# Columns of maxima become rows by a VectorE transpose and GpSimd copies, in place of TensorE products with the identity

## The chip, the cores and the metric

The kernel runs on one core of one Trainium2 chip. The metric is the device time in microseconds of one execution; times are medians of several runs. Engines are named as in the profile: PE is TensorE's matmul and PEld its weight load, DVE is VectorE, ACT is ScalarE, POOL is GpSimd, SP is SyncE, whose queue issues most DMAs.

## The reference

The input x has 4096 tokens of 256 features, all float32. There are two residual stages: causal attention with 16 heads of 16 features, then a feed-forward part with five linear maps.

```
def attn(x):                      # x: [1, 4096, 256]
    q, k, v = split(x @ w_attn + b_attn, 3)      # 16 heads of 16
    logits = q @ k^T * 16 ** -0.5
    logits = where(causal, logits, -inf)
    return softmax(logits) @ v @ w_proj + b_proj

def ffn(x):
    h = silu((x @ w1^T) * s1) * ((x @ w2^T) * s2)
    h = gelu((h @ h1^T) * sh1)
    h = gelu((h @ h2^T) * sh2)
    return (h @ w3^T) * s3

x = x + layernorm(attn(layernorm(x)))
x = x + layernorm(ffn(layernorm(x)))
```

The softmax subtracts each query's true maximum. The change touches only how this maximum gets from where it is found to where it is used.

## The kernel before, in words

**Tiling.** Queries come in 8 blocks j of 512 tokens (QB), each of 4 tiles t of 128 (P). The 16 heads form 4 groups g of 4; a group is two pairs pr of two heads i. The work of the attention is a list of 32 items (j, g), counted here from 0. Item (j, g) has 4(j+1) steps kt, one for each 128 keys up to the diagonal.

**Two passes.** An item needs its maxima before its scores. `MaxUnit` computes, with queries on the partitions, 128 x 512 logits of two heads into two PSUM banks `pm` (L596; three such banks in a ring) and reduces each on DVE to one column of `mx` (L630; L634 with the causal mask on the diagonal; if `hold` is set, ACT first copies one bank to SBUF at L615 and DVE reduces the copy at L619). After the last unit of an item, DVE takes the maximum over key blocks with the sign turned, `neg` (L647), rounds it, `high` (L653), and writes `high` and the rest `neg - high` into columns of `mcol` (L657, L658): 4 heads, 2 parts, 4 query tiles. `ScoreUnit` then computes the logits the other way round, with keys on the partitions and queries along the free axis (L701): a first product with q and k and a second that adds the negative maximum, as a product of a matrix of ones with a row tile `mrow`, which must hold the maxima along the free axis. ACT takes the exponential of two heads at once (L716), POOL zeroes what lies above the diagonal with an affine select in the last four steps of an item (L721), and four products with the values (L751, each issued twice in the trace) add to `av`, one step later than their scores.

**Columns to rows, before.** `to_rows` (L661) multiplies each of the four 128 x 128 tiles of `mcol` with the identity on PE (L666) into a PSUM tile `pmt`, taken from the ring of two that the scores use as well, and ACT copies it to SBUF as `mrow` (L675). In `mcol` the two heads of a pair lie 64 columns apart, so that in `mrow` they lie on the two halves of the partitions, where the two products of L701 read them; all other columns are zero. `ones[pr]` (L405) has ones in the four rows that belong to pair pr.

**Order.** All engines run in program order; the order is written out by hand (L893 on). In step kt of item n the program issues the first `MaxUnit` of a pair, the two `ScoreUnit`s, the second `MaxUnit`, the values of the step before, and then `rows_of`, background work (`bg.pace`: layernorm and projections of other blocks) and a piece of `halve_weights` on POOL (L786). The maxima run about one item ahead of the scores and three steps more (`LEAD`); in items with g < 3 of the middle blocks up to four pairs more are drawn ahead beside the background work (`unit_beside`, L857). `issue` (L842) puts a finished item into `rows_due` with the time `now + 4`, where `now` goes up by 2 per step, so its rows are made two steps later. `lent` notes that ACT was used beside the exponentials; the next step then does not hold.

Of the kernel before, what the change touches and what calls it, by code (L numbers as in the profile page):

```python
# [10 lines left out]
F32 = mybir.dt.float32  # L11
F32R = mybir.dt.float32r
AF = mybir.ActivationFunctionType
ALU = mybir.AluOpType
AX = mybir.AxisListType
PSUM = bass.MemoryType.PSUM

P = 128
QB = 512
NT = QB // P  # L20
NEG = -1.0e30
# [46 lines left out]
def sandwich_kernel(  # L68
# [19 lines left out]
    nc = tc.nc  # L88
# [6 lines left out]
    G = H // 4  # L95
    NB = S // QB
    DC = D // P
    FC = F // P
    SCALE = HD ** -0.5

    const = ctx.enter_context(tc.tile_pool(name="const", bufs=1))
    lent = []
# [4 lines left out]
    stat = ctx.enter_context(tc.tile_pool(name="stat", bufs=3))  # L107

    def rows(src, j):
        return src[j * QB : (j + 1) * QB, :].rearrange("(t p) d -> p t d", p=P)  # L110

    def load_block(j, src=x):
        t = xpool.tile([P, NT, D], F32, tag="x", name=f"x{j}")
        nc.sync.dma_start(out=t, in_=rows(src, j))
        return t


    x1 = [
        scratch.tile([QB, D], F32, tag=f"x1_{j}", name=f"x1_{j}") for j in range(NB)
    ]  # L120
# [10 lines left out]

    ident = const.tile([P, P], F32, tag="ident", name="ident")
    make_identity(nc, ident)
# [54 lines left out]
    def piece(tag, name, dtype=F32):  # L188
        return pieces.tile([P, QB], dtype, tag=tag, name=name)

# [12 lines left out]
    def load_pieces(src, tiles):  # L203
        for (c, o), t in tiles.items():
            nc.sync.dma_start(
                out=t.bitcast(F32), in_=src[c * P : (c + 1) * P, o * QB : (o + 1) * QB]
            )
# [139 lines left out]
    with ExitStack() as actx:  # L347
        aw = actx.enter_context(tc.tile_pool(name="aw", bufs=1))
        kv = actx.enter_context(tc.tile_pool(name="kv", bufs=1))
        wk2 = actx.enter_context(tc.tile_pool(name="wk2", bufs=2))  # L350
# [10 lines left out]
        def two_banks(name):  # L361
            return ps_s.tile([P, 2, QB], F32, tag="s", name=name)
# [17 lines left out]
        for d in range(DC):  # L380
# [10 lines left out]
        nc.scalar.dma_start(out=bqk, in_=b_attn[0 : 2 * D].rearrange("(s p) -> p s", p=P))  # L391
        nc.vector.tensor_scalar(bqk[:, 0:DC], bqk[:, 0:DC], SCALE, None, ALU.mult)

        two = aw.tile([P, 2], F32, tag="two", name="two")
        nc.vector.tensor_reduce(
            two,
            ident.rearrange("p (i pr e) -> p pr i e", i=2, pr=2)[:, :, :, 0:2],
            AX.XY,
            ALU.add,
        )  # L400
        identr = aw.tile([P, P], F32R, tag="identr", name="identr")
        nc.vector.tensor_copy(identr, ident)
        ones = [aw.tile([P, P], F32R, tag=f"ones{pr}", name=f"ones{pr}") for pr in range(2)]
        for pr in range(2):
            nc.vector.tensor_copy(ones[pr], two[:, pr : pr + 1].to_broadcast([P, P]))  # L405
# [16 lines left out]
        vb, qT, mT = [], {}, {}  # L422
# [161 lines left out]
        class MaxUnit:  # L584
# [19 lines left out]
            def finish(self, hold=False):  # L604
                j, g, t, c, pr = self.at
                n = self.n
                heads = list(self.ps.items())
                if hold:


                    h, ps = heads.pop(0)
                    held = const.tile(
                        [P, QB], F32, tag=f"xT0{'hl'[c % 2]}", name=f"held_{j}_{g}_{t}_{c}"
                    )
                    nc.scalar.copy(held[:, 0:n], ps[:, 0:n])  # L615
                    heads.append((h, held))
                for h, ps in heads:
                    if not self.diagonal and hold and ps is held:
                        nc.vector.tensor_scalar(  # L619
                            held[:, 0:n],  # L620
                            held[:, 0:n],
                            -3.0e38,
                            None,
                            ALU.max,
                            ALU.max,
                            accum_out=self.mx[:, h, c : c + 1],
                        )
                        continue
                    if not self.diagonal:
                        nc.vector.tensor_reduce(  # L630
                            self.mx[:, h, c : c + 1], ps[:, 0:n], AX.X, ALU.max
                        )
                        continue
                    nc.vector.tensor_tensor_reduce(  # L634
                        out=ps[:, 0:n],
                        in0=ps[:, 0:n],
                        in1=mask[:, QB - n : QB],
                        scale=1.0,
                        scalar=-3.0e38,
                        op0=ALU.add,  # L640
                        op1=ALU.max,
                        accum_out=self.mx[:, h, c : c + 1],
                    )
                if not (self.diagonal and pr == 0):
                    return False
                neg, mcol = self.neg, self.mcol
                nc.vector.tensor_reduce(  # L647
                    neg[:, t, :], self.mx[:, :, 0 : j + 1], AX.X, ALU.max, negate=True
                )
                if t < NT - 1:  # L650
                    return False
                high = stat.tile([P, NT, 4], F32R, tag="high", name=f"high_{j}_{g}")
                nc.vector.tensor_copy(high, neg)  # L653

                col = mcol.rearrange("p t (i pr e) -> p t pr i e", i=2, pr=2)
                by_pair = [a.rearrange("p t (pr i) -> p t pr i", pr=2) for a in (neg, high)]
                nc.vector.tensor_copy(col[:, :, :, :, 0], by_pair[1])  # L657
                nc.vector.tensor_tensor(col[:, :, :, :, 1], *by_pair, ALU.subtract)  # L658
                return True

            def to_rows(self):  # L661

                j, g = self.at[:2]
                ps = two_banks(f"pmt_{j}_{g}")[:, 0, :]
                for t in range(NT):
                    nc.tensor.matmul(  # L666
                        ps[:, t * P : (t + 1) * P],
                        lhsT=self.mcol[:, t, :],
                        rhs=identr,
                        start=True,  # L670
                        stop=True,
                    )
                mrow = wk2.tile([P, QB], F32R, tag="mrow", name=f"mrow_{j}_{g}")
                lent.append(True)
                nc.scalar.copy(mrow, ps)  # L675
                mT[j, g] = mrow

        class ScoreUnit:

# [85 lines left out]
                        bg.add(("project", j), project(j, room), PROJECT)  # L765


        mcols = [aw.tile([P, NT, P], F32R, tag=f"mcol{i}", name=f"mcol{i}") for i in range(2)]
        for mcol in mcols:
            nc.gpsimd.memset(mcol.bitcast(F32), 0.0)  # L770

        PW = 256
        fit = aw.tile([P, PW], F32, tag="fit", name="fit")
# [66 lines left out]
        rows_due = deque()  # L840

        def issue(unit, **how):  # L842
            unit.products()
            done = unit.finish(**how)
            if done is True:
                rows_due.append((now + 4, unit))
            return done

        def rows_of(limit):
            while rows_due and rows_due[0][0] <= limit:  # L850
                rows_due.popleft()[1].to_rows()

# [2 lines left out]
        def unit_beside():  # L857
            j, g = item
            if not begun_pair and 1 <= j < NB - 1 and g < G - 1 and len(ahead) < NT:
                begun_pair.extend(next(stream))  # L860
                ahead.append(1)
            if begun_pair:
                issue(MaxUnit(*begun_pair.pop(0)))
# [6 lines left out]
        ps = two_banks("pb")[:, 0, 0:D]  # L870
        for c in range(DC):
            nc.tensor.matmul(
                ps,
                lhsT=bv[:, c : c + 1].to_broadcast([P, P]),
                rhs=wp[:, c, :],
                start=(c == 0),
                stop=(c == DC - 1),
# [10 lines left out]
        while issued < first[1] + LEAD:  # L888
            for args in next(stream):
                issue(MaxUnit(*args))  # L890
            issued += 1
        rows_of(now + 4)
        for n, (j, g) in enumerate(items):  # L893
            if n + 2 < len(items):
# [21 lines left out]
            for kt in range(count[n]):  # L916
# [7 lines left out]
                if pairs:  # L924
                    unit = MaxUnit(*pairs[0][0])
# [16 lines left out]
                if j > 0 and kt % 4 == 2 and kt < NT * j:  # L942
                    next(halving, None)
            rows_of(now + 2)
            if n == len(items) - 2:
                count_low()
# [253 lines left out]
```

## Time and profile before

| | us |
|---|---|
| median of 3 runs | 2411.34 |
| lowest and highest | 2408.91, 2411.72 |
| the profiled execution | 2409.51 |
| its span, first to last instruction | 2407.8 |
| PE busy | 2332.1 |
| DVE busy | 1772.5 |
| ACT busy | 1460.8 |
| POOL busy | 564.3 |
| attention, until about | 1750 |

Busy time is the time in which an engine has at least one instruction under way. A row of the profile names the line, the engine, the operation, the tiles written and read, shapes and count; behind the bar stand the busy time, the mean duration, and the idle time of the engine just before, with what ended it. Rows of the timeline start with the time since the span began and the duration; instructions of one kind in a row are merged. The value in brackets is the idle time before, with the instruction that ended it.

### The profile page before, as it was taken

The page shows a single profiled execution, that of the slowest core. Times are in us where ns is not written, and L with a number is a line of the kernel's source. Part 1 is how long each engine was busy: PE and PEld are TensorE (multiplying, and loading weights), DVE is VectorE, ACT ScalarE, POOL GpSimd, SP SyncE. Part 2 cuts the span into 40 slices and gives each one's busy share as a digit, 9 for nine tenths or more (in the row PEclk, how much of TensorE's full clock was granted, in tenths as well). Part 3 has the DMA queues.
Part 4 walks back from the last instruction along what each step waited for, and adds up shares of the span by engine and source line. Part 5 has one row for each costly group of instructions (what it writes and reads, how often), then busy time and mean ns, then how long its engine had stood idle before and what let it go on. Part 6 is the DMA issues. An engine that isn't in the chain of part 4 may idle for free.

```text
span 2407.8 us, 40664 instructions
## 1 busy us (share of the span) xinstructions
PE 2332.1 (97%) x15237; PEld 1413.8 (59%) x15237; DVE 1772.5 (74%) x4053; ACT 1460.8 (61%) x1995; POOL 564.3 (23%) x898
## 2 busy tenths in 40 slices
PE   4899999999999999999999999999999999999998
PEld 2545545545554555455555455544388888888887
DVE  1667897997997999799999998987056546544653
ACT  1437776777786888688789887976822222222221
POOL 2324343333343224322422323000001100000000
PEclk8879999999999999999999999999999999999999
DMA  4443434334334323524223232111031000000000
GB/s 143 162 147 132 152 119 154 122 96 139 103 115 131 109 91 106 167 84 151 75 70 94 80 111 65 61 58 62 1 104 45 27 1 18 18 16 3 18 9 11
DMA packets 134831, 202.77 MB, mean 84 GB/s; under 512 B 14913, under 2 KB 59585, under 8 KB 134625
## 3 DMA queue, kind: packets, MB, share of 16 engines
q1 hardware_dynamic: 132672, 198.75, 25.5%
q8 instruction: 122, 2.00, 0.3%
q10 hardware_dynamic: 1776, 1.18, 0.3%
q14 instruction: 85, 0.69, 0.1%
q0 software_dynamic: 176, 0.15, 0.1%
HBM read 137.91 MB, written 62.13 MB: 83 GB/s over the span
## 4 chain that ended last, share of the span: by engine, by line
PE 84%; DVE 7%; DMA 3%; issue 2%; POOL 2%; ACT 1%; SPq 1%; ACTq 0%; POOLq 0%; DVEq 0%
PE av L751 20%; PE z L1056 19%; PE s L701 18%; PE pm L596 15%; DVE mx L630 3%; PE za L1056 2%; PE zb L1056 2%; PE pyf L1138 2%; DVE pm L634 2%; PE py L254 1%; PE pk L439 1%; PE pmt L666 1%; DMA k<-k 1%; SPq L462 1%; DMA k<-lok 1%
## 5 line engine op out<-in xcount | busy, mean ns | idle before, releaser
L716 ACT ACTIVATE e<-s 128x1024 f32<-128x1024 f32 (+3 forms) x1175 | 1038.2, 936 | 168.1 <-PE s L701 155.5
L630 DVE TENSOR_REDUCE mx<-pm 128x1 f32<-128x512 f32 x1545 | 989.0, 685 | 136.7 <-PE pm L596 103.5
L596 PE MATMUL pm<-k,q 64*128 64x512 f32 (+3 forms) x2304 | 587.8, 443 | 22.6 <-DVE mx L630 9.4
L596 PEld LDWEIGHTS pm<-k,q 64*128 64x128 f32 x2304 | 310.3, 187 | 502.8 <-DVE mx L630 349.7
L751 PE MATMUL av<-e,v 128*32 128x512 f32 (+3 forms) x4608 | 579.2, 573 | 1.8 <-POOL e L721 1.7
L701 PE MATMUL s<-q,k 64*128 64x512 f32 (+3 forms) x2304 | 467.1, 390 | 5.7 <-ACT xT L547 1.2
L701 PE MATMUL s<-mrow,ones 64*128 64x512 f32 (+3 forms) x2304 | 454.3, 380 | 0.0
L1123 ACT ACTIVATE fb<-z,sh 128x512 f32<-128x512 f32 x128 | 88.3, 690 | 364.6 <-PE z L1056 339.3
L634 DVE CUSTOM_DVE_ANT_0 pm<-pm,mask 128x128 f32<-128x128 f32 (+3 forms) x506 | 236.6, 514 | 72.1 <-PE pm L596 68.3
L701 PEld LDWEIGHTS s<-q,k 64*128 64x128 f32 x2304 | 231.4, 187 | 76.6 <-issue 18.2
L701 PEld LDWEIGHTS s<-mrow,ones 64*128 64x128 f32 x2304 | 236.1, 187 | 36.3 <-ACT mrow L675 0.5
L721 POOL TENSOR_SCALAR_AFFINE_SELECT e<-e 128x256 f32<-128x256 f32 x256 | 102.7, 409 | 583.7 <-ACT e L716 580.6
L1056 PE MATMUL z<-hb_0h,h 128*128 128x512 f32 x512 | 199.3, 389 | 0.0
L1056 PE MATMUL z<-hb_0l,h 128*128 128x512 f32 x512 | 199.2, 389 | 0.0
L615 ACT COPY held<-pm 128x512 f32<-128x512 f32 x253 | 148.6, 588 | 52.1 <-PE pm L596 30.2
L751 PEld LDWEIGHTS av<-e,v 128*32 128x32 f32 x4608 | 91.8, 108 | 147.2 <-issue 131.2
L176 POOL TENSOR_TENSOR rstd<-ve,neghalf 128x4 f32<-128x4 f32 (+1 forms) x22 | 20.8, 945 | 644.4 <-DVE ve L174 618.3
L619 DVE TENSOR_SCALAR_CACHE_REDUCE held<-held 128x512 f32<-128x512 f32 x247 | 167.0, 676 | 0.0
L1023 DVE CAST hb_1h<-fb 128x512 fp32r<-128x512 f32 x64 | 27.3, 427 | 155.3 <-ACT fb L1123 155.3
L1100 ACT ACTIVATE sl<-za,s 128x512 f32<-128x512 f32 x64 | 44.1, 690 | 120.1 <-PE za L1056 60.9
L1056 PEld LDWEIGHTS z<-hb_0l,h 128*128 128x128 f32 x512 | 96.1, 188 | 19.9
L1056 PEld LDWEIGHTS z<-hb_0h,h 128*128 128x128 f32 x512 | 96.1, 188 | 19.9
(251 smaller groups left out, 2522.7 us busy)
## 6 DMA issues: line engine op xcount, KB each, us to landing
k<-k SPq DMA_DIRECT2D x288, 256.0 KB
q<-q SPq DMA_DIRECT2D x64, 256.0 KB
x<-in_x_dram SPq DMA_DIRECT2D x16, 512.0 KB
k<-hik SPq DMA_DIRECT2D x32, 256.0 KB
k<-lok SPq DMA_DIRECT2D x32, 256.0 KB
q<-hiq SPq DMA_DIRECT2D x32, 256.0 KB
q<-loq SPq DMA_DIRECT2D x32, 256.0 KB
avd<-av_sb SPq DMA_DIRECT2D x32, 256.0 KB
```

The lines of the kernel that those rows point to most:

```text
L596: nc.tensor.matmul(ps[:, 0:n], lhsT=qT[j, g][pr][r, t * P : (t + 1) * P], rhs=kT[G * j + g, c, pr][r, 0:n], start=True, stop=True,)
L615: nc.scalar.copy(held[:, 0:n], ps[:, 0:n])
L619: nc.vector.tensor_scalar(held[:, 0:n], held[:, 0:n], -3.0e38, None, ALU.max, ALU.max, accum_out=self.mx[:, h, c : c + 1],)
L630: nc.vector.tensor_reduce(self.mx[:, h, c : c + 1], ps[:, 0:n], AX.X, ALU.max)
L634: nc.vector.tensor_tensor_reduce(out=ps[:, 0:n], in0=ps[:, 0:n], in1=mask[:, QB - n : QB], scale=1.0, scalar=-3.0e38, op0=ALU.add, op1=ALU ...
L701: nc.tensor.matmul(self.ps[i][:, self.q0 :], lhsT=(self.k, ones[pr])[m][r, :], rhs=(qT[j, g][pr], mT[j, g])[m][r, self.q0 :], start=(m == ...
L716: nc.scalar.activation(e[:, at : at + n, q0:], ps[:, :, q0:], AF.Exp)
L721: nc.gpsimd.affine_select(out=at, in_=at, compare_op=ALU.is_ge, fill=0.0, base=0, pattern=[[0, 2], [1, P]], channel_multiplier=-1,)
L751: nc.tensor.matmul(self.av[h * HW : (h + 1) * HW, q0:], lhsT=vb[kt // NT][:, kt % NT, o : o + HW], rhs=es[h // 2][:, h % 2, q0:], start=(k ...
L1056: nc.tensor.matmul(ps, lhsT=w[c], rhs=single(part[:, c, :]), start=(c == 0 and i == 0), stop=(c == kc - 1 and i == parts - 1),)
L1123: nc.scalar.activation(h, z, AF.Gelu, scale=sc[:, oc : oc + 1])
L1138: nc.tensor.matmul(ps[:, 0:D], lhsT=single(part[:, c, t * P : (t + 1) * P]), rhs=(w3_r if halves else w3_sb)[:, c, :], start=(c == 0 and i ...
```

## The change

DVE now transposes the columns in 32 x 32 blocks and POOL puts the blocks into their places. `mcol` shrinks to 32 columns per query tile, of which 8 are used; the transpose turns each block of 32 queries by 32 columns in place, so that queries 32b to 32b+31 end up on partitions 32b to 32b+31 as rows of columns. Four copies on POOL, one for each b, move 32 partitions by 128 elements into 32 partitions of a row tile; they are done twice, for partitions 0 to 31 and 64 to 95 (i = 0 and 1), the first four after the step in which the maxima are finished, the others one step later. The row tiles are now two fixed ones, zeroed once. Both halves hold the rows of all four heads; `ones` is rearranged so that each half picks its own. The identity in the products' rounded type (`identr`), the four products, the copy on ACT and its entry in `lent` are gone.

```diff
+        halves = aw.tile([P, 2, 2], F32, tag="halves", name="halves")
+        for i in range(2):
+            at = (P // 2 + 4) * i
+            nc.vector.tensor_reduce(
+                halves[:, i, :],
+                ident[:, at : at + 4].rearrange("p (pr e) -> p pr e", pr=2),
+                AX.X,
+                ALU.add,
+            )
         two = aw.tile([P, 2], F32, tag="two", name="two")
-        nc.vector.tensor_reduce(
-            two,
-            ident.rearrange("p (i pr e) -> p pr i e", i=2, pr=2)[:, :, :, 0:2],
-            AX.XY,
-            ALU.add,
-        )
-        identr = aw.tile([P, P], F32R, tag="identr", name="identr")
-        nc.vector.tensor_copy(identr, ident)
+        nc.vector.tensor_tensor(two, halves[:, 0, :], halves[:, 1, :], ALU.add)
...
-                col = mcol.rearrange("p t (i pr e) -> p t pr i e", i=2, pr=2)
+                col = mcol[:, :, 0:8].rearrange("p t (i pr e) -> p t pr i e", i=2, pr=2)
                 by_pair = [a.rearrange("p t (pr i) -> p t pr i", pr=2) for a in (neg, high)]
                 nc.vector.tensor_copy(col[:, :, :, :, 0], by_pair[1])
                 nc.vector.tensor_tensor(col[:, :, :, :, 1], *by_pair, ALU.subtract)
+                self.turned = stat.tile([P, NT, TB], F32, tag="turned", name=f"turned_{j}_{g}")
+                nc.vector.transpose(self.turned, mcol.bitcast(F32))
                 return True
 
-            def to_rows(self):
+            def to_rows(self, i):
                 j, g = self.at[:2]
-                ps = two_banks(f"pmt_{j}_{g}")[:, 0, :]
-                for t in range(NT):
-                    nc.tensor.matmul(
-                        ps[:, t * P : (t + 1) * P],
-                        lhsT=self.mcol[:, t, :],
-                        rhs=identr,
-                        start=True,
-                        stop=True,
-                    )
-                mrow = wk2.tile([P, QB], F32R, tag="mrow", name=f"mrow_{j}_{g}")
-                lent.append(True)
-                nc.scalar.copy(mrow, ps)
-                mT[j, g] = mrow
+                mT[j, g] = mrow = mrows[g % 2]
+                at = slice(i * P // 2, i * P // 2 + TB)
+                row = mrow[at, :].rearrange("c (t b q) -> c t b q", t=NT, q=TB)
+                for b in range(P // TB):
+                    nc.gpsimd.tensor_copy(row[:, :, b, :], self.turned[b * TB : (b + 1) * TB, :, :])
...
-        mcols = [aw.tile([P, NT, P], F32R, tag=f"mcol{i}", name=f"mcol{i}") for i in range(2)]
-        for mcol in mcols:
-            nc.gpsimd.memset(mcol.bitcast(F32), 0.0)
+        mcols = [aw.tile([P, NT, TB], F32R, tag=f"mcol{i}", name=f"mcol{i}") for i in range(2)]
+        mrows = [aw.tile([P, QB], F32R, tag=f"mrow{i}", name=f"mrow{i}") for i in range(2)]
+        for zero in mcols + mrows:
+            nc.gpsimd.memset(zero.bitcast(F32), 0.0)
...
             if done is True:
-                rows_due.append((now + 4, unit))
+                rows_due.extend(((now + 2, unit, 0), (now + 4, unit, 1)))
             return done
 
         def rows_of(limit):
             while rows_due and rows_due[0][0] <= limit:
-                rows_due.popleft()[1].to_rows()
+                _, unit, i = rows_due.popleft()
+                unit.to_rows(i)
```

`TB` is 32.

More of the change, by code (lines that the diff above doesn't have):

```diff
@@ L18 @@
 P = 128
+TB = 32
 QB = 512
```

## The prediction

> **What bounds the kernel now.** I read the views in this order: busy time by stage, the groups by form, then the timeline of one engine at a time around single row products. The stages first (time, then busy us and instructions of PE, PEld, DVE, ACT, POOL, the granted clock, DMA):
>
> ```profile
> core 0: us, PE busy (x) PEld busy (x) DVE busy (x) ACT busy (x) POOL busy (x), PEclk, DMA share, GB/s
> 300.00:600.00 300.00, 294.30 (x2134) 150.67 (x2134) 257.70 (x614) 224.10 (x321) 110.75 (x183) 1.00 0.39 126
> 600.00:900.00 300.00, 298.25 (x2204) 154.46 (x2200) 269.45 (x607) 236.28 (x322) 100.36 (x158) 1.00 0.35 110
> ```
>
> In the attention PE is never idle and DVE is busy nine tenths of the time; POOL has two thirds free. But a busy PE may be waiting inside its queue, so the place itself decides. Here is the end of the maxima of item 30 (a pair of query block and head group; 32 of them, counted from 0). DVE, then PE, then POOL:
>
> ```profile
> 1579.05 0.18 DVE L658 TENSOR_TENSOR mcol<-neg,high 128x16 fp32r<-128x16 f32 x1
> 1579.13 2.48 DVE L630 TENSOR_REDUCE mx<-pm 128x1 f32<-128x512 f32 x4
> 1582.41 0.69 DVE L630 TENSOR_REDUCE mx<-pm 128x1 f32<-128x512 f32 x1 [0.81 <-PE pm L596]
> ```
> ```profile
> 1579.87 0.49 PE L596 MATMUL pm<-k,q 64*128 64x512 f32 x1 [0.40 <-DVE mx L630]
> 1580.30 1.06 PE L751 MATMUL av<-e,v 128*32 128x512 f32 x8
> 1581.29 0.66 PE L666 MATMUL pmt<-identr,mcol 128*128 128x128 f32 x4
> 1581.88 0.50 PE L596 MATMUL pm<-k,q 64*128 64x512 f32 x2
> ```
> ```profile
> 1579.93 0.41 POOL L721 TENSOR_SCALAR_AFFINE_SELECT e<-e 128x256 f32<-128x256 f32 x1 [1.13 <-ACT e L716]
> 1580.63 0.41 POOL L721 TENSOR_SCALAR_AFFINE_SELECT e<-e 128x256 f32<-128x256 f32 x1 [0.29 <-ACT e L716]
> 1583.38 0.92 POOL L721 TENSOR_SCALAR_AFFINE_SELECT e<-e 128x256 f32<-128x256 f32 x2 [2.34 <-ACT e L716]
> ```
>
> The row product occupies PE from 1581.29 to 1581.88, 0.59 us, and right behind it DVE has been idle for 0.81 us, waiting for PE: here PE sets the pace. But 1.4 us earlier PE waited 0.40 us for DVE, because a pm bank (three in the ring) was not yet reduced. Two engines take turns within one item, and the change takes from one and gives to the other.
>
> **Removed: PE.** Four 128x128 products per item. The next group's mean is 298 ns each, but they overlap: start to start of what surrounds them gives 0.59 us per item. In items 0 and 4, at a lower granted clock, it is 1.05 us (79.69 to 80.74, 152.62 to 153.66).
>
> ```profile
> L666 PE MATMUL pmt<-identr,mcol 128*128 128x128 f32 x128 | 22.2, 298 | 1.7 <-DVE mcol L658 1.7
> ...
> L139 DVE BATCH_NORM_STATS2 bn<-x 128x6 f32<-128x256 f32 x40 | 16.6, 416 | 0.0
> ...
> L456 POOL CAST hik<-fullk 128x512 fp32r<-128x512 f32 x14 | 8.6, 612 | 90.8 <-ACT fullk L448 90.8
> ```
>
> [...] The rows say 0.59 us, 19 us in all: matmuls in a queue overlap, and the row decides. So the prize is small, [...].
>
> **Removed: ACT and a PSUM slot.** The copy of the row (0.59 us, 32 times) goes. ACT waited for PE before it (45.9 us over 30 copies), so it was not late. Without the copy the kernel no longer notes ACT as lent, and in steps off the diagonal the next step may hold a pm bank through ACT instead (0.59 us): one for one, nothing. The score products no longer share the ring of two with the row (5.5 us of waits, 24 times, weight loads mostly hidden): nothing counted.
>
> **Added: DVE.** One transpose of 128 elements per partition. From bn_stats above, 416 ns for 256 elements; the reduction of 512 elements takes 0.62 us start to start, its row says 0.685, so 0.065 overlaps, and an element costs 1.05 ns (685 minus 416 over 256). So 128 elements last about 0.28 us and hold the engine about 0.22. It depends on L658 just in front (0.18 us), while the reduction now behind it started after 0.08: 0.12 us of waiting more. Together 0.35 us per item. [...] Bounds: 0.22, if the wait hides, and 0.77, if it held DVE like the dearest near row (L634 with the mask, 512 elements, 0.65 start to start); I take 0.35, as bn_stats is the nearest row.
>
> **Added: POOL.** Eight copies of 32 partitions by 128 elements. No row shows fewer than 128 partitions or a move between partitions. Casts of 512 and 256 elements take 612 and 398 ns, so 128 make 0.29 us; an affine select of 128x128 takes 0.31. POOL rows go by elements per partition, so I expect no gain from 32 partitions. Bounds: 0.15 us (the small memset of the value block) and 1.28 (L458, POOL's dearest plain row). I take 0.30, as cast and select are the nearest, so 1.2 us for each of two fours. Behind them in POOL's queue stand the affine selects of the diagonal steps, and for those wait the av products.
> In item 30's place: transpose done at 1579.05 + 0.2 + 0.28 = 1579.55, first four to 1580.75, the two selects (ready from 1579.93) to 1581.6, second four to 1582.8, the next selects at 1583.38 unhindered. The delayed selects are needed at 1583.35 (av of that step, 1583.59 now). Cover of 2 us, so no cost. Background work on POOL (halving weights, projection) is pushed by 2.4 us per item, and away from the diagonal the rows have 12 us until use.
>
> **Start.** The sum over ident in two halves against a 128x128 cast: a fifth of a us, at a time when DVE waited 11.6 us for data. Two more memsets on POOL against shorter ones: under 1 us at 7 us, behind the loads. Both nothing, at worst 1 us.
>
> **The sum, item by item** (from the timeline around all 32):
> - Items 8 to 16, 18, 20, 21, 24, 25, 28 to 30, seventeen: DVE stalls PE after the maxima, PE leads later. Gain 0.59 - 0.35 = 0.24 each: 4.1 us.
> - Items 1, 2, 3, 5, 7, 17, 19, seven: DVE goes idle, or PE does not wait on it, after the maxima; the transpose mostly hides. 0.5 each: 3.5 us.
> - Items 0 and 4: 1.05 - 0.35 = 0.7 each: 1.4 us.
> - Items 6, 22, 23, 26, 27, five: DVE runs through, so PE without the product only waits for a bank. In item 22 it could start at 958.04 instead of 958.63, but the second bank comes free at 958.50, with the transpose 958.85. Loss 0.2 each: -1.0 us.
> - Item 31: its maxima end at 1674.95 and its first row is used at 1676.55. Transpose and eight copies last until 1675.3 + 2.7 = 1678.0. Loss 1.4 us.
>
> ```profile
> 957.88 3.77 DVE L630 TENSOR_REDUCE mx<-pm 128x1 f32<-128x512 f32 x6
> 961.87 0.69 DVE L630 TENSOR_REDUCE mx<-pm 128x1 f32<-128x512 f32 x1 [0.21 <-PE pm L596]
> ```
>
> Sum 6.6 us. The profiled execution took 2409.51 us (span 2407.8 and 1.7 around it), so 2402.9; its distance of 1.83 us below the median of the runs, 2411.34, carries over: 2404.7.
>
> **Rivals.**
> 1. *POOL is late* (slower). The copies cost c each, and the selects behind them hold up the av products. In the place above: second four begin at 1579.55 + 4c + 0.9, the next step's first select ends at 1580.9 + 8c, and av needs it at 1585.84. The limit is c = 0.62; from there each 0.1 us costs 0.8 in the eleven items whose copies fall among diagonal steps (1 to 3, 8, 12, 16, 20, 24, 28 to 30), 8.8 us in all. The gain of 6.6 is gone at c = 0.70; c = 0.9 gives 2404.7 + 24 = 2429, c = 0.8 gives 2420. For it: a move between partitions is shown nowhere, and POOL slows beside DVE at times (one tensor_scalar at 954.16 took 0.99 us, mean 0.58). Against: every simple POOL row of 128 elements is at 0.2 to 0.3.
> 2. *DVE takes it all* (no change). It costs in 24 items (17, 2 and 5 of the sum). At 0.62 us per transpose, 0.27 more each, the 6.6 us are gone and the time is 2411; at the bound of 0.77 it is 2415. For it: DVE is at 90%, and PE already waits for it in seventeen items.
> 3. *The transpose hides and PE gets everything*: 0.59 in 24 more items, plus 6 us or so: 2398. Against it stand the 0.40 us that PE waits for DVE now.
>
> **How the numbers follow.** A measurement can tell about 0.2% (4.8 us) from no change. The likeliest case, 50%, runs from 2401 (0.22 per transpose: 24 times 0.13 less) to 2409 (0.48, elements at half the pace, and 1 us of the start): five sixths of it is faster by over 0.2%. Rival 1: 28%, nearly all slower. Rival 2: 15%, two thirds within 0.2%, the rest slower. Rival 3: 7%, faster. Together faster 0.49, same 0.20, slower 0.31. The range runs from rival 3 to c = 0.85; the likeliest case's own is 2401 to 2409.
>
> **What would show it.** The transpose's row at 0.28 to 0.31 us and the POOL copies at 0.30 bear out the costs. The PE gap before pm in the seventeen items should grow from 0.40 to about 0.5 to 0.75, and the DVE gap behind should shrink from 0.81 to about 0.6 or less. Waits of av for POOL's selects (10.3 us now) well above that, or waits of s for mrow from POOL outside item 31, mean rival 1. A transpose above 0.5 us and no faster PE mean rival 2. I am wrong altogether if the copies pass 0.62 us.

## The result, and the profile after

The changed kernel takes 2417.61 us (median of 7 runs, 2414.95 to 2420.06), the kernel before, run beside it, 2410.14 us (7 runs, 2408.28 to 2412.25). The ratio is 1.0032, 95% interval [1.0021, 1.0042]: slower by 7.7 us, where 6.6 us less was forecast. The profiled execution took 2417.61 us, its span 2415.9. Shares below are differences of ratios times 2410 us; places are read from single profiled executions, which differ among themselves by some us.

What was costed came out as costed. The transposes in the view of the tile `turned` (minimum, median, maximum in ns), then the copies in the groups of the page:

```profile
L663 DVE STREAM_TRANSPOSE turned<-mcol x32: 311/311/314, 74.6 to 1680.3; 128x128 f32<-128x128 f32 x32
```
```profile
L675 POOL CAST mrow<-turned 32x128 fp32r<-32x128 f32 x256 | 73.0, 285 | 170.0 <-DVE turned L663 96.5
```

A transpose of these 4-byte data takes 0.311 us, where my estimate from the rows was 0.28. A copy takes 0.285 us where I took 0.30. The end of the maxima of item 30, on DVE, PE and POOL, also went much as worked out:

```profile
1583.13 0.18 DVE L661 TENSOR_TENSOR mcol<-neg,high 128x16 fp32r<-128x16 f32 x1
1583.42 0.31 DVE L663 STREAM_TRANSPOSE turned<-mcol 128x128 f32<-128x128 f32 x1
1583.66 2.45 DVE L633 TENSOR_REDUCE mx<-pm 128x1 f32<-128x512 f32 x4
1586.32 1.29 DVE L633 TENSOR_REDUCE mx<-pm 128x1 f32<-128x512 f32 x2 [0.22 <-PE pm L599]
```
```profile
1584.37 0.49 PE L599 MATMUL pm<-k,q 64*128 64x512 f32 x1 [0.82 <-DVE mx L633]
1584.79 1.06 PE L750 MATMUL av<-e,v 128*32 128x512 f32 x8
1585.78 0.50 PE L599 MATMUL pm<-k,q 64*128 64x512 f32 x2
```
```profile
1583.80 1.26 POOL L675 CAST mrow<-turned 32x128 fp32r<-32x128 f32 x4 [0.91 <-DVE turned L663]
1585.13 0.77 POOL L720 TENSOR_SCALAR_AFFINE_SELECT e<-e 128x256 f32<-128x256 f32 x2
1585.96 1.28 POOL L675 CAST mrow<-turned 32x128 fp32r<-32x128 f32 x4
1587.35 0.83 POOL L720 TENSOR_SCALAR_AFFINE_SELECT e<-e 128x256 f32<-128x256 f32 x2
```

The reductions behind L661 start 0.53 us after it instead of 0.08, PE's gap before `pm` is 0.82 us instead of 0.40 (a little over the 0.5 to 0.75 of the forecast), the next pair of `pm` follows av without the product, and DVE's gap fell from 0.81 to 0.22 us. The selects are delayed, but the products of av do not wait for them. Here the item is 0.2 us shorter, as forecast. The waits show where something else happened (us in total, times, longest); the last line is that of the kernel before:

```profile
POOL mrow L675 <- DVE turned L663: 96.5, 21, 24.8
...
PEld av L750 <- POOL e L720: 16.7, 45, 1.8
```
```profile
PEld av L751 <- POOL e L721: 10.3, 34, 1.3
```

POOL stood up to 24.8 us at a copy that waited for its transpose, and the weight loads of av waited for POOL's selects 45 times instead of 34.

To find the places I take how long every item lasts, from the start of its scores to that of the next, after minus before. Items 11 to 20 are shorter by 0.02 to 0.5 us each. Item 21 is longer by 1.7, items 24 to 26 by 0.9, 0.9 and 0.7, and item 31 by 2.9. And item 8 starts only 0.2 us earlier than before, where the forecast comes to about 4 us. What is lost in item n comes from the rows of item n + 1, except in item 31, the last, which waits for its own. Items 8, 9, 28 and 30 are longer too, by 1.9, 0.7, 0.6 and 1.2, and item 27 is shorter by 1.7. In all of these but item 9 the two kernels also differ in the time that TensorE's clock was at half (3.4, 2.3 and 3.4 us more, in item 27 2.3 less); the last section comes back to it.

### The profile page after: what moved, and what is told of

It reads as the page before. It is cut to its first block, busy times and chain, and to the rows that moved or that the text cites. A ratio compares the mean times of both kernels' runs of the same rounds, so it can differ in the third digit from the quotient of the medians.

```text
span 2415.9 us, 40749 instructions
## 1 busy us (share of the span) xinstructions
PE 2321.4 (96%) x15109; PEld 1401.7 (58%) x15109; DVE 1779.1 (74%) x4087; ACT 1442.7 (60%) x1964; POOL 633.8 (26%) x1156
## 3 DMA queue, kind: packets, MB, share of 16 engines
q10 hardware_dynamic: 1776, 1.18, 0.2%
## 4 chain that ended last, share of the span: by engine, by line
PE 81%; DVE 7%; DMA 4%; POOL 3%; issue 2%; ACT 2%; SPq 1%; ACTq 0%; POOLq 0%; DVEq 0%
PE av L750 19%; PE z L1057 19%; PE s L700 17%; PE pm L599 14%; DVE mx L633 3%; PE za L1057 2%; PE zb L1057 2%; PE pyf L1139 2%; DVE pm L637 2%; PE py L255 1%; DMA k<-k 1%; PE pk L442 1%; ACT e L715 1%; SPq L465 1%; POOL mrow L675 1%
## 5 line engine op out<-in xcount | busy, mean ns | idle before, releaser
L599 PE MATMUL pm<-k,q 64*128 64x512 f32 (+3 forms) x2304 | 594.4, 444 | 34.3 <-DVE mx L633 20.2
L1024 DVE CAST hb_1h<-fb 128x512 fp32r<-128x512 f32 x64 | 27.3, 427 | 155.7 <-ACT fb L1124 155.7
L675 POOL CAST mrow<-turned 32x128 fp32r<-32x128 f32 x256 | 73.0, 285 | 170.0 <-DVE turned L663 96.5
```

What stands on the lines that cost most here:

```text
L599: nc.tensor.matmul(ps[:, 0:n], lhsT=qT[j, g][pr][r, t * P : (t + 1) * P], rhs=kT[G * j + g, c, pr][r, 0:n], start=True, stop=True,)
L675: nc.gpsimd.tensor_copy(row[:, :, b, :], self.turned[b * TB : (b + 1) * TB, :, :])
```

## The experiments

All start from the changed kernel; each ratio is against the kernel before on the same chip. First the parts.

**Without transposes and copies.**
```diff
-                self.turned = stat.tile([P, NT, TB], F32, tag="turned", name=f"turned_{j}_{g}")
-                nc.vector.transpose(self.turned, mcol.bitcast(F32))
...
-                for b in range(P // TB):
-                    nc.gpsimd.tensor_copy(row[:, :, b, :], self.turned[b * TB : (b + 1) * TB, :, :])
```


> The changed kernel without the transposes and without the copies: the row tiles stay zero, so the maxima are not subtracted. It shows what taking the four products and the ACT copy away is worth by itself. Theory (the gains before item 8 are absorbed by waits for the key transfers, the later ones are kept): 0.59 us in some 19 items from item 8 on and little elsewhere, 11 to 12 us below the kernel before, ratio 0.995; the starts of items 3 and 7 do not move. Rival (my prediction's step, early gains kept too): about 17 us below, ratio 0.993, with items 4 and 8 starting about 4 us earlier. Second rival (the removal is worth nothing, PE was not the bound): ratio 1.000.

Measured: 2396.80 us, ratio 0.9941 [0.9927, 0.9955], 14.2 us below. Most items from 11 on gain about 0.6 us each, those with a busy DVE (21, 22, 25, 26) 0.1 to 0.2. Items 8, 10 and 30 lose 1.9, 1.5 and 0.9, each with 3.4 us at half clock that the kernel before does not have there; in item 27 it is the other way round, and it gains 2.2. Item 8 starts 6.7 us earlier: the early gain is there, and my guess after the result, that waits for the key transfers absorb it, falls.

**With the transposes, without the copies.**
```diff
-                for b in range(P // TB):
-                    nc.gpsimd.tensor_copy(row[:, :, b, :], self.turned[b * TB : (b + 1) * TB, :, :])
```


> The changed kernel with the transposes, without the copies: the row tiles stay zero, so the maxima are not subtracted. Theory DVE (each transpose holds up the reductions behind it by about 0.37 us and PE with them): about 8 to 9 us above the run without rows, some 3 us below the kernel before. Theory queue (the loss comes from POOL's copies, which wait at the head of POOL's queue with background work and affine selects behind them): at most 3 us above the run without rows.

Measured: 2407.09 us, 0.9987 [0.9980, 0.9993], 11 us above the run without rows. Items with 0.6 us of gain keep 0.1 to 0.35. The theory of DVE holds for its size, but it is only half of what is lost.

**Copies straight from mcol, no transposes.**
```diff
-                self.turned = stat.tile([P, NT, TB], F32, tag="turned", name=f"turned_{j}_{g}")
-                nc.vector.transpose(self.turned, mcol.bitcast(F32))
+                self.turned = mcol.bitcast(F32)
```


> The changed kernel with the copies taken straight from mcol, without the transpose: the rows hold untransposed columns, so wrong maxima are subtracted, with the same waits of POOL for DVE but 0.37 us earlier. Theory queue: 7 to 10 us above the run without rows, of which 2 to 3 us lie in item 31, where PE waits for the rows, and 1 us each in items 21, 24, 25 and 26. Theory DVE: at most 3 us above the run without rows, nearly all of it in item 31.

Measured: 2408.21 us, 0.9994 [0.9987, 1.0001], 13 us above the run without rows. Against that run it loses 1.5, 1.2, 0.7 and 0.6 us in items 21, 24, 25 and 26, 3.0 in item 31, 4.5 before item 8 and 0.9 in item 9; elsewhere little. So the copies cost as much as the transposes, in few places. The theories of the queue and of DVE both hold, side by side: 14.2 us saved, some 11 spent on DVE, some 11 more on POOL.

**The same copies without a wait.**
```diff
-                self.turned = stat.tile([P, NT, TB], F32, tag="turned", name=f"turned_{j}_{g}")
-                nc.vector.transpose(self.turned, mcol.bitcast(F32))
+                self.turned = still
...
+        still = aw.tile([P, NT, TB], F32, tag="still", name="still")
+        nc.gpsimd.memset(still, 0.0)
```


> The changed kernel without the transpose, with the copies taken from a tile of zeros that is written once, so the maxima are not subtracted: POOL has the same copies at the same places of its queue, but never waits for DVE. Theory (waiting at the head of POOL's queue is what costs): 2 to 4 us above the run without rows, 2399 to 2401. Rival (POOL's occupied time is what costs): as the copies taken from mcol, 11 us above the run without rows, 2408.

Measured: 2402.55 us, 0.9970 [0.9961, 0.9979]: 7 us above the run without rows and 6 below the copies that wait, between the two expectations. The profile parts it by place: items 21, 24 to 26 and 31 lose at most 0.15 us against the run without rows; item 8 starts 2.7 us later. The profiled execution took 2398.80 us, 3.8 less than the median, so it holds only half of the 7 us, and where the other half lies is not shown. At the late places the wait is the whole cost; before item 8 POOL's time itself seems to count too.

**The queue's order.** Item 25, on POOL in the kernel before (first block), then on POOL and PE in the changed kernel; the lines left out are of the same halving piece (L804 to L807):

```profile
1232.70 0.40 POOL L804 CAST wh<-wc 128x256 fp32r<-128x256 f32 x1 [6.36 <-DMA wc<-in_h_t_dram]
...
1253.60 0.41 POOL L721 TENSOR_SCALAR_AFFINE_SELECT e<-e 128x256 f32<-128x256 f32 x1 [17.92 <-ACT e L716]
```
```profile
1253.85 1.26 POOL L675 CAST mrow<-turned 32x128 fp32r<-32x128 f32 x4 [24.80 <-DVE turned L663]
1255.17 0.40 POOL L804 CAST wh<-wc 128x256 fp32r<-128x256 f32 x1
...
1257.41 0.73 POOL L807 TENSOR_TENSOR fit<-fit,wc 128x256 f32<-128x256 f32 x1
1258.21 1.28 POOL L675 CAST mrow<-turned 32x128 fp32r<-32x128 f32 x4
1259.56 1.53 POOL L720 TENSOR_SCALAR_AFFINE_SELECT e<-e 128x256 f32<-128x256 f32 x4
```
```profile
1259.20 0.74 PE L599 MATMUL pm<-k,q 64*128 64x512 f32 x2
1260.03 1.41 PE L750 MATMUL av<-e,v 128*32 128x512 f32 x8
```

In the kernel before, the four operations of that halving piece (L804 to L807) ran from 1232.70 to 1235.68, and POOL then waited 17.92 us for the first select: it was that far ahead of the other engines. Now the first four copies stand in front of the piece and wait for DVE; the piece is done after them, the second four behind the piece, and the selects of two steps come in one burst. The av products, 1.06 us otherwise, take 1.41. The experiment issues the piece ahead of `rows_of`:

```diff
+                if j > 0 and kt % 4 == 2 and kt < NT * j:
+                    next(halving, None)
                 rows_of(now)
                 bg.pace(count[n] - kt + count[n] * max(G - 2 - g, 0))
-                if j > 0 and kt % 4 == 2 and kt < NT * j:
-                    next(halving, None)
```


> The changed kernel, complete, with the piece of weight halving of a step issued ahead of the row copies instead of behind them. Theory queue: POOL no longer holds the halving piece behind copies that wait for DVE, so the selects of the diagonal are on time in items 21, 24, 25 and 26; 3 to 5 us below the changed kernel, ratio about 1.0015. Theory DVE: no change, ratio 1.003.

Measured: 2410.69 us, 0.9998 [0.9989, 1.0008], 8 us below the changed kernel. Items 21 and 24 to 26 lose about as much as with the transposes alone, 3.7 us less than in the changed kernel, and item 8 starts 3.1 us earlier than there. The theory of the queue had 3 to 5 us, for the late items alone. POOL in the same place:

```profile
1247.79 2.59 POOL L675 CAST mrow<-turned 32x128 fp32r<-32x128 f32 x8 [14.63 <-DVE turned L663]
1251.71 0.41 POOL L720 TENSOR_SCALAR_AFFINE_SELECT e<-e 128x256 f32<-128x256 f32 x1 [1.34 <-ACT e L715]
1252.55 0.41 POOL L720 TENSOR_SCALAR_AFFINE_SELECT e<-e 128x256 f32<-128x256 f32 x1 [0.43 <-ACT e L715]
```

POOL still waits 14.63 us at the copies, but nothing that matters stands behind them: the selects wait for ACT again. The wait cost only through what was queued behind it.

**The last item.** The wait of PE for the rows of item 31 in the changed kernel:

```profile
1681.28 0.50 PE L700 MATMUL s<-q,k 64*128 64x512 f32 x2
1682.02 0.50 PE L700 MATMUL s<-mrow,ones 64*128 64x512 f32 x1 [0.24 <-POOL mrow L675]
1683.36 0.79 PE L700 MATMUL s<-mrow,ones 64*128 64x512 f32 x1 [0.84 <-POOL mrow L675]
```

and the stretch behind it (columns as in the prediction: the granted clock is the third figure from the end):

```profile
1682.50:1689.30 6.80, 5.96 (x30) 2.39 (x29) 0.00 (x0) 4.42 (x6) 0.72 (x3) 0.50 0.54 204
```

```diff
+                    put = nc.scalar.copy if i and (j, g) == (NB - 1, G - 1) else nc.gpsimd.tensor_copy
-                    nc.gpsimd.tensor_copy(row[:, :, b, :], self.turned[b * TB : (b + 1) * TB, :, :])
+                    put(row[:, :, b, :], self.turned[b * TB : (b + 1) * TB, :, :])
```


> The changed kernel, complete, with the second four copies of the last item (31) on ACT, which is idle there, beside POOL's first four. Theory (PE's wait for the rows, and the half clock that follows it, make the 2.9 us lost in item 31): the wait of s for the rows shortens by 1.3 us, and item 31 by 1.3 to 3 us; 2415 to 2416, ratio 1.0022 to 1.0027. Rival (the clock window comes whatever the wait): 1.3 us at most in item 31.

Measured: 2413.41 us, 1.0026 [1.0014, 1.0037]; the interval overlaps that of the changed kernel, so the total settles nothing. The place shows more. PE with the copies shared:

```profile
1679.87 0.50 PE L701 MATMUL s<-q,k 64*128 64x512 f32 x2
1680.61 0.50 PE L701 MATMUL s<-mrow,ones 64*128 64x512 f32 x2 [0.23 <-POOL mrow L676]
```

The second half no longer waits, the clock is at half for 3.4 us instead of 6.8, as it was for 3.4 us (from 1676.7) in the kernel before, and item 31 loses 0.3 us instead of 2.9. That the shorter wait made the shorter stretch is not shown, and other runs speak against it. In the last run below the copies are shared in the same way and PE waits for no row in item 31; yet the clock is at half for 6.8 us, and the item loses 1.7:

```profile
1674.42:1681.25 6.83, 6.79 (x34) 2.65 (x36) 0.40 (x2) 4.87 (x8) 0.51 (x2) 0.50 0.67 251
```

With the transposes alone, where no row is waited for either, it was at half for 6.8 us as well (from 1669.4).

**The transpose one step later.** With the halving first, the transpose is issued with the first four copies at `now + 4`, and the second four at `now + 6` (the edit of the halving is not shown again):

```diff
-                self.turned = stat.tile([P, NT, TB], F32, tag="turned", name=f"turned_{j}_{g}")
-                nc.vector.transpose(self.turned, mcol.bitcast(F32))
                 return True
...
             def to_rows(self, i):
                 j, g = self.at[:2]
+                if i == 0:
+                    self.turned = stat.tile([P, NT, TB], F32, tag="turned", name=f"turned_{j}_{g}")
+                    nc.vector.transpose(self.turned, self.mcol.bitcast(F32))
...
-                rows_due.extend(((now + 2, unit, 0), (now + 4, unit, 1)))
+                rows_due.extend(((now + 4, unit, 0), (now + 6, unit, 1)))
```


> The changed kernel, complete, with the halving piece first and with the transpose and both fours of copies one step later, so that DVE first does the reductions of the step behind the maxima. Theory (the 10 us of the transposes come from the place where DVE is already late, and would vanish into DVE's gap one step later): 5 to 8 us below the run with the halving first alone, about 2404, ratio 0.9973. Rival (DVE's time is on the path wherever it is spent): no change against that run, 2410.7, ratio 1.000.

Measured: 2408.56 us, 1.0000 [0.9991, 1.0009]: no change in total, as the rival had it. By place the theory holds, and something hides it. From the start of item 8 to the end this run gains 7.3 us against the kernel before, while the run with the halving first alone loses 4.5 there; but it starts item 8 2.6 us later than the kernel before, not 3.3 earlier. In items 0 to 5 the score products now wait for rows (3.3 us, 4 times, between 80 and 190 us): their items have 4 to 8 steps, and one more step of delay is too much.

**All three edits** (halving first, late transpose, last copies shared).

> The changed kernel, complete, with halving first, the late transpose and the last item's second four copies on ACT. If the three places are independent: the time of the late transpose less 1.3 to 3 us, about 2402, ratio 0.9965. If the clock or the weight transfers set the end of the attention anyway: the same as with the late transpose alone.

Measured: 2405.13 us, 0.9983 [0.9976, 0.9989], 4 us below the late transpose alone, and the first complete kernel below the kernel before. Item 31 loses 0.2 us where it lost 1.9 with the late transpose alone; the other 2 us are within what the two intervals leave open.

**The late transpose from item 8 on** (the edit against the run with all three).
```diff
+                if j < 2:
+                    self.turned = stat.tile([P, NT, TB], F32, tag="turned", name=f"turned_{j}_{g}")
+                    nc.vector.transpose(self.turned, mcol.bitcast(F32))
...
-                if i == 0:
+                if i == 0 and j > 1:
...
+                at = now + 2 * (unit.at[0] > 1)
-                rows_due.extend(((now + 4, unit, 0), (now + 6, unit, 1)))
+                rows_due.extend(((at + 2, unit, 0), (at + 4, unit, 1)))
```


> The changed kernel, complete, as with all three edits, but items 0 to 7 keep the transpose and the copies at the changed kernel's places (their items are 4 to 8 steps long, so that rows one step later came after their use). Theory (the late transpose gains 9 to 11 us from item 8 on and loses 5 to 7 us before it): 4 to 7 us below the run with all three edits, about 2399, ratio 0.996. Rival (what moved before item 8 was the clock's chance windows, not late rows): as the run with all three edits, ratio 0.998.

Measured: 2398.97 us, 0.9955 [0.9942, 0.9969], 10.8 us below the kernel before, 18.6 below the changed one and 6.7 below all three edits, as the theory had it. DVE, then PE, around the maxima of item 30:

```profile
1570.04 0.18 DVE L661 TENSOR_TENSOR mcol<-neg,high 128x16 fp32r<-128x16 f32 x1
1570.13 2.48 DVE L633 TENSOR_REDUCE mx<-pm 128x1 f32<-128x512 f32 x4
1572.52 0.30 DVE L674 STREAM_TRANSPOSE turned<-mcol 128x128 f32<-128x128 f32 x1
1572.82 3.77 DVE L633 TENSOR_REDUCE mx<-pm 128x1 f32<-128x512 f32 x6
```
```profile
1570.87 0.49 PE L599 MATMUL pm<-k,q 64*128 64x512 f32 x1 [0.41 <-DVE mx L633]
```

The transpose lies where DVE used to wait for PE, and PE's gap is back at 0.41 us. The same 0.31 us of DVE costs 0.4 us per item at one place and next to nothing four reductions later: items 11 to 20 last as long as without rows, within 0.15 us. What is still lost against that run in the late items is 1.3 us in item 24, where av waits for POOL's selects (0.9 us) with every late transpose, and 0.2 to 0.5 in items 21, 25, 26 and 31.

**Early copies on DVE** (items 0 to 7, on top of the last run).
```diff
-                    put = nc.scalar.copy if i and (j, g) == (NB - 1, G - 1) else nc.gpsimd.tensor_copy
+                    put = nc.vector.tensor_copy if j < 2 else nc.gpsimd.tensor_copy
+                    put = nc.scalar.copy if i and (j, g) == (NB - 1, G - 1) else put
```


> As the run before, complete, but in items 0 to 7 DVE itself makes the eight copies, and POOL none. Theory (before item 8 it is POOL's queue, with the layernorm and the key halves of the next block behind the copies, that loses 3 to 4 us): item 8 starts 1 to 4 us earlier than in the run before; ratio 0.995. Rival (DVE's time counts there as much): eight copies of about 0.2 us in eight items cost up to as much again, item 8 starts no earlier.

Measured: 2409.02 us, 0.9995 [0.9985, 1.0004], 10 us above the last run. Item 8 starts 9.5 us later than in it, so the rival holds: 64 copies of 0.22 us (median) are 14 us of DVE, and most of that shows. DVE is no way out there.

## Why the prediction was wrong

- **Removed from PE:** right in size. The terms for the product alone add up to 17 us (17 and 7 times 0.59, 2 times 1.05, 5 times about 0.15); the run without rows shows 14.2, interval 10.8 to 17.6, with 0.6 us in most items where 0.59 was read from the queue.
- **Added to DVE:** right in size. Terms of 0.35 us in 24 items and 0.1 in seven make 9; measured 11 (the two intervals together leave 7 to 15). One part was off: I let the transpose hide in item 17's rows, and they lost the same 0.4 us as the rest.
- **Added to POOL:** this step failed. It said: "Cover of 2 us, so no cost. Background work on POOL (halving weights, projection) is pushed by 2.4 us per item, and away from the diagonal the rows have 12 us until use." Measured, the copies on top of the transposes cost 10.8 us (0.9987 to 1.0032): by the profiles 4 before item 8, 4 in items 21 and 24 to 26, and 2.4 in item 31. I counted POOL's busy time behind a copy that is ready, worked it through at item 30 alone, and gave the rows a deadline but not the work behind them. POOL works through its queue in the order of issue and had been far ahead: a copy issued in the step in which the maxima are issued stood at the head of the queue up to 24.8 us before its transpose was done. The halving piece that stood behind it had been done 18 us early before; now it fell into the selects. With that piece in front of the copies, the complete kernel gained 8 us.
- **Item 31:** the wait was named, at 1.4 us (with 2.7 us for eight copies, where eight times 0.30 are 2.4); PE's waits for the rows came to 1.1 (0.24 and 0.84). The item lost 2.9. The rest fits the 3.4 us more at half clock, worth 1.7 at most by the estimate in the last section, a term that the sum does not have.
- **Rival 1** ended on the right side for a reason it did not give. It let lateness be decided by a copy's duration, from 0.62 us on; the copies took 0.285. The sign was lost in the order of the queue. The places were others, too: the four items that the copies lengthened by 0.5 to 1.5 us hold the rows of items 22 and 25 to 27, none of which is among its eleven; of those from item 8 on, six of eight show less than 0.1 us, and in the other two the clock differs as well. (A small misreading in the bounds: L458 is not POOL's dearest plain row, L180 takes 1.34 us. Nothing rested on it.)
- **Before item 8:** the terms for the rows of items 0 to 8 add up to 3.9 us of gain; the removal alone gives 6.7 at the start of item 8, the changed kernel keeps 0.2. Transposes take 2.6 of it, copies 3.9, and 3.1 came back when the halving went first. But these are single executions: two runs with the same edits up to there (halving first, and late from item 8 on) start item 7 2.0 us apart. What part of this is the work itself and what the clock (below), the runs do not settle.

## What to carry to other kernels

When a wait is put on an engine that is mostly idle, ask what the engine had been doing ahead of time: everything that is queued behind the wait loses its lead (17.9 us here, in item 25), and it lands where the next deadline is. Issue such work behind what has no need of it, and move a small operation on a busy engine to the place where that engine waits for others. Work such sums at several kinds of places, not at the most regular one: over half of what the copies cost lay in five items out of 32.

## What the runs showed of the hardware beyond that

The granted clock went to half in stretches (the windows of the expectations). In the clock records of the profiled executions of the kernels before and after, sixteen of the eighteen stretches are 3.41 us long or a multiple of it (6.83, 17.07, 20.48, 23.89); the other two are the last of each execution and run on past the last instruction. Ahead of the 6.8 us of item 31 in the changed kernel PE was busy for 2.89 of 3.41 us and then for 1.18 of 3.42, with a longest gap of 2.35 us; what brings such a stretch on is not shown:

```profile
1675.67:1679.08 3.41, 2.89 (x28) 1.18 (x24) 3.41 (x9) 0.75 (x3) 1.25 (x4) 1.00 0.30 99
1679.08:1682.50 3.42, 1.18 (x4) 0.45 (x4) 2.14 (x10) 0.00 (x0) 1.57 (x6) 1.00 0.82 268
```

What a stretch costs can be read in item 30: the changed kernel and the run with the last copies shared are the same code there but for those copies, only the former has 3.4 us at half in it, and it takes 1.6 us more. Half of 3.4 is 1.7, which I take as an estimate of the most that a stretch of this length costs.

Between 90 and 260 us the sum of these stretches goes with the start of item 8 against the kernel before: 17.1 us at half and 6.7 us earlier without rows, 20.5 and 4.0 with the copies that never wait, 23.9 and 4.1 with transposes alone, 27.3 and 0.0 before and 0.2 earlier after, 34.1 and 4.0 later with all three edits, 37.5 and 7.8 later with the early copies on DVE; the five other runs lie in between, in the same order. From end to end these are 20.5 us more at half, worth 10.2 us at most by the same estimate, where the start of item 8 moves by 14.5: the stretches are not all of it.

The clock goes with the time of whole runs, too. Of the runs of the kernel before made beside the experiments, the seven with a mean granted clock of 0.980 or 0.981 took 2414.8 us on average, the fifteen at 0.985 and above 2407.5. Six of the seven runs of the changed kernel lie at 0.980 to 0.982 and took 2418.1. So, as an estimate from these means, 3 to 4 of the 7.7 us are left at the same clock, and the rest goes with the clock. Whether gaps of PE that the change makes bring the stretches on, or part of them are chance, stays open: in none of these runs was the clock held fixed.

A GpSimd cast of 32 partitions by 128 elements into another quarter of the partitions takes 0.285 us, about what the line through the full-width casts of 256 and 512 elements (398 and 612 ns) gives for 128, 0.29; the same move took 0.22 us on DVE (median) and 0.29 on ACT.
